# Layer 3 of a fused conv-and-sequence kernel: rows of the spatial map asked for one row block ahead, in image 0 on POOL's DMA queue

## The chip, the cores and the metric

The kernel runs on one core of a Trainium2 chip. The metric is the device time of one execution in microseconds (us), as the median of several executions. One execution is also recorded by the hardware profiler; its own time stands beside its span below.

## The reference, cut to what matters

Four layers are computed one after the other on a batch of 4 images of 96 channels and 64x64 pixels: a selective-scan sequence block, a depthwise convolution with a scan, a neighbourhood-attention block, and a deformable convolution with attention from the spectrum. The change touches the fourth alone:

```python
mag = jnp.abs(jnp.fft.rfft2(x, norm='ortho'))
ca = sigmoid(...)                # from mag: one factor per image and channel
sa = sigmoid(...)                # from mean, l2 and mag: one factor per image and pixel
y = x * ca * sa
magy = jnp.abs(jnp.fft.rfft2(y, norm='ortho')).mean(1, keepdims=True)
freq_e = jax.image.resize(magy, (b, 1, h, w), method='bilinear')
aux = jnp.concatenate([y, coord, freq_e], 1)
offset = _conv(aux, off_w, off_b, (1, 1))
gate = sigmoid(_conv(relu(_conv(aux, dg1_w, dg1_b, (1, 1))), dg2_w, dg2_b))
y_base = _conv(y, base_w, base_b, (1, 1))
sampled = _grid_sample_taps(y, px, py)      # 9 taps, bilinear, at pixel + offset
y_def = einsum('bcthw,oct->bohw', sampled, def_w) + def_b
z = (1 - gate) * y_base + gate * y_def
return relu(batch_norm(z) + x)
```

`sa` has one value per pixel and is the same for all channels.

## The kernel before, in words

An image lies in SBUF as 96 channels (partitions) by 4096 pixels. Layer 3 cuts it into 8 row blocks of 512 pixels (`NB` = 512, `NN` = 8), and numbers the blocks of all images m = 0 to 31. Nothing is reordered by a scheduler in this part: `tc.manual_schedule()` keeps each engine's instructions in the order in which the Python code emits them. Steps are written as generators, and two tables say which generator takes a step when.

The spatial map `sa` of an image is computed in pixel rows on 64 partitions (`sr_acc`), written to DRAM (`sa_d`, L1823), and read back by row blocks.

`attended(b, n)` makes row block n of y for image b. Its first step asks for the 512 values of the block, copied to 96 partitions (`sab`, L1883, 192 KB), and multiplies the block in place by `ca` and `sab` on DVE (L1885). Then `row_steps` transposes the block on PE (`tp`, L1610), copies it to SBUF (`xT`, L1615: on DVE in image 0, on ACT in the others), multiplies it by the row transform on PE (`fa`, L1626), and ACT copies the result to `f1` (L1634). After the copy to `xT`, eight DMAs on SyncE's queue (SP) write the block into a table in DRAM in which every pixel holds its four neighbours (L1892). `sab` has two buffers. `xT` has three, which it shares with `fT` (L1653, the copies of the column transform, `columns`; their matmuls are L1646 and L1657 and their sums L1663).

The first part of the layer is `front`. It runs a table of slots over the spectra of the four images, the maps, and `attended` of image 0: its blocks start at slots 42, 44, ... 56, with `columns` of image 2 and `described` of image 3 between them. POOL has nothing to do there.

The second part is a loop over u = 0 to 127, four u for each block m. It is called the gather stage here. For each u, POOL issues nine indirect DMAs (L2010, `gathered`) that fetch 128 pixels x 9 taps from the table, each 128 x 1536 B, into `sm` (three buffers). DVE weights and adds the neighbours (L2027 to L2031, `weighted`, for u-1), PE transposes the sums and ACT copies them (L2048 to L2051). `mixed(m)` multiplies them by the deformable weights (`yd`, L2060) and DVE combines the result (`z`, L2065). The addresses for block m+1 come meanwhile: `guides` (PE `go`, L1933, ACT L1946), `offsets` (PE L1954, DVE L1961 to L1990, with `om` on L1987), which POOL's next gathers wait for. `attended(b, n)` of images 1 to 3 is spread over this loop, one block every two u in the first half of image b-1. On DVE a cycle in that half has this order: offsets, attended, weighted, weighted, attended, weighted, z, weighted, offsets.

Of the kernel before, what the change touches and what calls it, by code (L numbers as in the profile page):

```python
# [10 lines left out]
F32 = mybir.dt.float32  # L11
I32 = mybir.dt.int32
AF = mybir.ActivationFunctionType
ALU = mybir.AluOpType
# [4 lines left out]
B, C, H, W = 4, 96, 64, 64  # L19
L = H * W  # L20
NB = 512
# [1808 lines left out]
def layer3(k, X, aux, out):  # L1830

    tc, nc, ins = k.tc, k.nc, k.ins
    with ExitStack() as es:
        wp = es.enter_context(tc.tile_pool(name="l3w", bufs=1))
        dram = es.enter_context(tc.tile_pool(name="l3d", bufs=1, space=DRAM))
        ca = wp.tile([C, B], F32, name="ca")
        sa_d = dram.tile([B, L], F32, name="sa_d")
# [26 lines left out]
        wk = es2.enter_context(tc.tile_pool(name="l3k", bufs=2))  # L1864
# [3 lines left out]
        NN, NJ = L // NB, 4  # L1868
# [2 lines left out]
        go, ix, cw, g, yb, sm, sd, sT = {}, {}, {}, {}, {}, {}, {}, {}  # L1871

        pairs = (("stp", "smm"), ("tp", "cv"))
        f1 = {}

        def attended(b, n, tags=None):

            table = tables[b % 2]
            s = slice(n * NB, n * NB + NB)
            if n == 0:  # L1880
                f1[b] = spec.begin()
            sab = wk.tile([C, NB], F32, name="sab")
            nc.sync.dma_start(sab, sa_d[b : b + 1, s].partition_broadcast(C))  # L1883
            y = X[b][:, s]
            nc.vector.scalar_tensor_tensor(y, y, ca[:, b : b + 1], sab, ALU.mult, ALU.mult)  # L1885
            yield
            for yT in spec.row_steps(f1[b], 4 * n, y, None, tags):
                if yT is not None:
                    for h2 in range(2):
                        for q in range(4):  # L1890
                            r, c = 8 * n + h2 + 1 - q // 2, 1 - q % 2
                            nc.sync.dma_start(  # L1892
                                table[r : r + 7 : 2, c : c + W, q].rearrange("r w c -> w r c"),
                                yT[64 * h2 : 64 * h2 + 64],
                            )
                yield
# [184 lines left out]
        def front(pool):  # L2081
# [7 lines left out]
            def chains(kind, b, ats):  # L2089
                for n, at in enumerate(ats):  # L2090
                    tags = pairs[at % 2]
                    if kind == "rows":
                        start(at, 3, described(b, n, pool, tags))
                    elif kind == "attended":
                        start(at, 4, attended(b, n, tags))
                    else:
                        start(at, 4, columns(b, FS[n], tags))
# [33 lines left out]
        with tc.manual_schedule():  # L2131
# [16 lines left out]
            for b in range(1, B):  # L2148
                u = NN * NJ * (b - 1)
                for n in range(NN):  # L2150
                    spread(2 * (u + 2 * n) + 1, 4, attended(b, n))
                u += 2 * NN + 1
                for i, f0 in enumerate(FS):
                    spread(2 * (u + i), 4, columns(b, f0))
                spread(2 * (u + len(FS) + 1), 4, frequency(b))
# [18 lines left out]
        for b in range(B):  # L2174
            for at in range(0, L, T):
                s = slice(at, at + T)
# [38 lines left out]
```

## Time and profile before

| | |
|---|---|
| median of 12 runs | 8195.92 us (8175.35 to 8217.66) |
| profiled execution, its own time | 8199.86 us |
| its span on the core | 8197.6 us |
| mean granted TensorE clock | 0.795 |
| busy PE, DVE, ACT, POOL | 71%, 71%, 48%, 57% of the span |
| layer 3, `front` up to the first gather | about 5640 to 6051 us of the span |
| gather stage | 6051 to 8117 us |
| `sab` requests on SP | 32, from 5823.8 to 7351.4 us |

A group line names the line of the code, the engine and the operation, what it writes and reads, how often, its busy time and mean, and the idle time of the engine just before it with what ended most of it. A wait line says who waited for whom: total us, number of times, longest. In a timeline a line starts with the start and the duration in us, and a bracket holds the idle time before it and what ended that. A releaser called "remote" is one that the profile could not put down to an instruction's end.

### The profile page before, as it was taken

Reading aid. Unit: us, or ns where it says so; the run is one execution under the profiler, and the core shown is the slowest. Engines: PE = TensorE matmul, PEld = TensorE weight load, DVE = VectorE, ACT = ScalarE, POOL = GpSimd, SP = SyncE. Lnnn points to the kernel's source line nnn. Section 1 sums busy time; section 2 is a strip of 40 time slices with the busy share of each in tenths; the row PEclk is TensorE's granted clock in tenths of the full one; section 3 lists DMA queues with packets and bytes.
Section 4 is the critical chain, followed back from the end, with each engine's and each line's share of the span. In section 5 each row is a group of like instructions: output and inputs, shape, how many; then the busy total and the mean of one; then the engine's idle time right before and its main releaser. Section 6 shows DMA issues by size and latency. Waiting matters only on the chain.

```text
span 8197.6 us, 76624 instructions
## 1 busy us (share of the span) xinstructions
PE 5826.7 (71%) x24090; PEld 2699.8 (33%) x24090; DVE 5788.8 (71%) x8127; ACT 3903.2 (48%) x7624; POOL 4693.4 (57%) x2915
## 2 busy tenths in 40 slices
PE   4777777777777776666788989897565566565553
PEld 1222222222222221422364646464542333233221
DVE  4999999999999998499763646454455565565555
ACT  4777776777677765344354646565321111111111
POOL 3888888888888887145442424243025555455453
PEclk8888888888888887777788888888677677777776
DMA  3322222332223332533200000000124344353333
GB/s 96 119 98 98 98 99 99 117 102 99 98 98 100 119 101 80 161 83 92 69 14 25 16 23 18 18 23 23 35 75 141 105 125 127 109 148 115 110 111 123
DMA packets 424411, 720.29 MB, mean 88 GB/s; under 512 B 188149, under 2 KB 190253, under 8 KB 419762
## 3 DMA queue, kind: packets, MB, share of 16 engines
q1 hardware_dynamic: 348710, 480.74, 19.0%
q0 software_dynamic: 73968, 227.47, 9.6%
q10 hardware_dynamic: 1328, 7.20, 0.2%
q8 instruction: 191, 3.13, 0.2%
q14 instruction: 214, 1.75, 0.1%
HBM read 567.04 MB, written 97.82 MB: 81 GB/s over the span
## 4 chain that ended last, share of the span: by engine, by line
PE 34%; DVE 26%; ACT 15%; issue 9%; another core or an unknown queue 8%; POOL 4%; DMA 3%; SPq 1%; DVEq 0%; ACTq 0%; POOLq 0%
DVE bt L604 6%; PE mm_ps L447 5%; DVE bt L577 3%; PE mm_ps L478 3%; PE yp L630 3%; PE sc_ps L1086 3%; ACT a_ps L588 3%; PE pT_ps L1135 2%; DVE prod L2027 2%; DVE sm L2028 2%; PE o_ps L1155 2%; POOL xc L472 2%; DVE lp L903 1%; PE yb_ps L1933 1%
## 5 line engine op out<-in xcount | busy, mean ns | idle before, releaser
L604 DVE TENSOR_TENSOR_SCAN bt<-a_ps,carry,bt 128x512 f32<-128x512 f32 x1536 | 1872.0, 1267 | 66.6 <-ACT a_ps L588 11.8
L613 POOL TENSOR_TENSOR bt<-bt,Cb 128x1536 f32<-128x1536 f32 x512 | 1758.3, 3444 | 200.1 <-ACT carry L612 178.7
L2010 POOL DMA_INDIRECT sm<-table,ix x1152 | 1097.5, 953 | 1319.2 <-DVE om L1987 493.9
L588 ACT ACTIVATE a_ps<-dR,w_l_A_log 128x512 f32<-128x512 f32 x1536 | 1039.9, 685 | 614.0 <-DVE bt L604 606.5
L577 DVE TENSOR_TENSOR bt<-xR,Bb 128x1536 f32<-128x1536 f32 x512 | 884.6, 1728 | 26.4 <-DMA xR<-spread 16.4
L2048 PE MATMUL sT_ps<-ident,sd 128*128 128x128 f32 (+1 forms) x896 | 223.0, 372 | 688.2 <-ACT sT L2049 344.5
L630 PE MATMUL yp<-bt,w_c_red 128*32 128x512 f32 x3072 | 596.1, 672 | 12.7 <-POOL bt L613 12.7
L570 PE MATMUL Bb<-dbl,w_c_seln 128*128 128x512 f32 x512 | 352.9, 777 | 326.3 <-DVE bt L577 326.3
L1123 POOL TENSOR_TENSOR p<-p,rs 128x392 f32<-128x392 f32 x384 | 312.0, 841 | 473.5 <-DVE rs L1121 404.8
L447 PE MATMUL mm_ps<-h,Wk 96*128 96x512 f32 x1024 | 481.2, 624 | 140.5 <-issue 87.3
L2065 DVE SCALAR_TENSOR_TENSOR z<-yd_ps,vec,yb 96x512 f32<-96x512 f32 x32 | 23.9, 746 | 530.3 <-remote 341.2
L2049 ACT COPY sT<-sT_ps 128x512 f32<-128x512 f32 (+1 forms) x256 | 122.0, 477 | 567.3 <-PE sT_ps L2048 241.5
L2048 PEld LDWEIGHTS sT_ps<-ident,sd 128*128 128x128 f32 (+1 forms) x896 | 132.7, 181 | 764.3 <-ACT sT L2049 373.8
L1110 ACT ACTIVATE p<-p,rs 128x196 f32<-128x196 f32 x768 | 342.7, 449 | 82.1 <-DVE rs L1100 81.9
L319 PE MATMUL bc_ps<-xs,w_l_bc 96*128 96x512 f32 x384 | 243.9, 769 | 184.1 <-DVE q L930 183.9
L447 PEld LDWEIGHTS mm_ps<-h,Wk 96*128 96x128 f32 x1024 | 198.1, 199 | 430.0 <-issue 430.0
L1946 ACT ACTIVATE go<-go_ps,w_l_go_b 18x512 f32<-18x512 f32 x32 | 21.7, 679 | 665.7 <-remote 503.9
L1933 PE MATMUL yb_ps<-X,w_l_base_w 96*128 96x504 f32 (+3 forms) x576 | 313.7, 710 | 0.3 <-ACT go L1947 0.3
L472 POOL TENSOR_TENSOR xc<-xc,gate 96x1024 f32<-96x1024 f32 x64 | 150.2, 2346 | 260.4 <-ACT carry L612 232.1
L1143 DVE COPY pT<-pT_ps 98x512 f32<-98x512 f32 x256 | 176.0, 687 | 148.8 <-PE pT_ps L1135 141.4
L2027 DVE TENSOR_TENSOR prod<-sm,cws 128x960 f32<-128x960 f32 (+1 forms) x256 | 270.8, 1058 | 6.7
L570 PEld LDWEIGHTS Bb<-dbl,w_c_seln 128*128 128x128 f32 x512 | 88.8, 217 | 552.8 <-DVE bt L577 492.9
(374 smaller groups left out, 13227.3 us busy)
## 6 DMA issues: line engine op xcount, KB each, us to landing
dR<-spread SPq DMA_DIRECT2D x384, 256.0 KB
xR<-spread SPq DMA_DIRECT2D x384, 256.0 KB
Cb<-out_states SPq DMA_DIRECT2D x256, 256.0 KB
spread<-w SPq DMA_DIRECT2D x128, 192.0 KB
spread<-dx SPq DMA_DIRECT2D x128, 192.0 KB
table<-xT SPq DMA_DIRECT2D x256, 96.0 KB
own<-vd SPq DMA_DIRECT2D x512, 36.8 KB
toep<-l_toep SPq DMA_DIRECT2D x12, 1536.0 KB
```

Of the source, the lines that this page charges most:

```text
L447: nc.tensor.matmul(p, Wk[:, i, t, hf], h[:, t : t + T], start=t == 0, stop=t == 3)
L570: nc.tensor.matmul(Bb, seln[:, nq], st["dbl"], start=True, stop=True)
L577: nc.vector.tensor_mul(bt, st["xR", hf, None], Bb.unsqueeze(1).to_broadcast([128, NG, T]))
L588: nc.scalar.activation(dec[n], st["dR", hf, q], AF.Exp, scale=A[:, i, nq, hf, q : q + 1])
L604: nc.vector.tensor_tensor_scan(t, dec.pop(n), t, carry_of(v)[:, q : q + 1], ALU.mult, ALU.add)
L613: nc.gpsimd.tensor_mul(bt, bt, st["Cb", nq].unsqueeze(1).to_broadcast([128, NG, T]))
L630: nc.tensor.matmul(st["yp", hf][32 * q : 32 * q + 32], red, bt[:, q], start=False, stop=nq == NQ - 1,)
L1110: nc.scalar.activation(ps[n][:, h, i], ps[n][:, h, i], AF.Exp, scale=-1.0, bias=rs[n][:, 0, h, i : i + 1], accum_out=rs[n][:, 1, h, i : i ...
L1933: nc.tensor.matmul(dv[:, r0:r1, c0:c1], w_[:, t], av[b][:ch, 8 * n + r0 + dy : 8 * n + r1 + dy, c0 + dx : c1 + dx], start=t == 4, stop=t == 8,
L2010: nc.gpsimd.indirect_dma_start(sm[u][:, t].rearrange("p q c -> p (q c)"), None, samples[m // NN % 2], bass.IndirectOffsetOnAxis(ap=ix[m][: ...
L2027: nc.vector.tensor_mul(p, v[:, :, 2:4], w_[:, :, 2:4])
L2048: nc.tensor.transpose(p[: e - 128 * q, q - q0], sf[:, 128 * q : e], k.ident)
```

## The change

A helper `fetch(b, n)` asks for the rows of one block. `attended(b, n)` now asks for block n+1 before it multiplies block n; with block 0 it asks for block 0 too. The requests of image 0 are issued by POOL's queue, those of images 1 to 3 by SP's as before. The multiplication takes the tile that was asked for earlier. The number of requests, their sizes and the buffers stay as they are.

```diff
-        f1 = {}
+        f1, sabs = {}, {}
+
+        def fetch(b, n):
+
+            t = sabs[b, n] = wk.tile([C, NB], F32, name="sab")
+            queue = nc.sync if b else nc.gpsimd
+            queue.dma_start(
+                t, sa_d[b : b + 1, n * NB : n * NB + NB].partition_broadcast(C)
+            )
...
             if n == 0:
                 f1[b] = spec.begin()
-            sab = wk.tile([C, NB], F32, name="sab")
-            nc.sync.dma_start(sab, sa_d[b : b + 1, s].partition_broadcast(C))
+                fetch(b, 0)
+            if n + 1 < NN:
+                fetch(b, n + 1)
             y = X[b][:, s]
-            nc.vector.scalar_tensor_tensor(y, y, ca[:, b : b + 1], sab, ALU.mult, ALU.mult)
+            nc.vector.scalar_tensor_tensor(
+                y, y, ca[:, b : b + 1], sabs.pop((b, n)), ALU.mult, ALU.mult
+            )
```

## The prediction

> **What bounds the kernel now.** I read the list of waits first, to see what the requests cost at all, and once more for the window of image 0 alone (5850 to 5960 us).
>
> ```profile
> DVE X L1885 <- DMA sab<-sa_d: 151.8, 23, 13.0
> POOL sm L2010 <- DVE om L1987: 493.9, 30, 33.2
> POOL sm L2010 <- DVE sd L2031: 125.7, 19, 13.8
> ```
>
> ```profile
> DVE X L1885 <- DMA sab<-sa_d: 60.6, 7, 8.9
> ```
>
> DVE stands 151.8 us before L1885 because the map's rows are not there; 60.6 us of it are seven waits in image 0, the other 91.2 us lie in the gather stage. The two POOL lines say that the gather queue stands still too, mostly for the addresses (`om`), less often for a free `sm` buffer (`sd`). Whether DVE's 91 us matter is decided there. Next the timeline of image 0, where one block gives way to the next.
>
> ```profile
> 5906.70 0.60 SPq L1883 DMA_DIRECT2D sab<-sa_d  x1
> 5909.94 0.75 DVE L1885 SCALAR_TENSOR_TENSOR X<-X,ca,sab 96x512 f32<-96x512 f32 x1 [8.56 <-DMA sab<-sa_d]
> 5910.74 0.90 PE L1610 MATMUL tp_ps<-ident,X 96*128 96x96 f32 x4 [4.85 <-DVE X L1885]
> 5911.69 0.56 DVE L1615 COPY xT<-tp_ps 128x384 f32<-128x384 f32 x1 [0.19 <-PE tp_ps L1610]
> 5912.27 5.24 SPq L1892 DMA_DIRECT2D table<-xT  x8
> 5917.56 0.60 SPq L1883 DMA_DIRECT2D sab<-sa_d  x1
> 5920.94 0.75 DVE L1885 SCALAR_TENSOR_TENSOR X<-X,ca,sab 96x512 f32<-96x512 f32 x1 [8.70 <-DMA sab<-sa_d]
> ```
>
> The request of a block stands in SP's queue behind the eight table stores of the block before (5.24 us of issuing), and its rows are usable 3.2 to 3.4 us after it is issued. All engines stand for that. The windows show how little else there is, against the stage after it:
>
> ```profile
> 5861.00:5945.00 84.00, 35.13 (x177) 30.00 (x178) 19.27 (x45) 9.91 (x25) 0.00 (x0) 0.60 0.37 83
> 6051.00:8117.00 2066.00, 1176.39 (x3419) 605.11 (x3417) 1170.06 (x1965) 287.73 (x647) 1097.28 (x1152) 0.71 0.43 122
> ```
>
> The columns are length, busy PE, PEld, DVE, ACT, POOL, clock, DMA share and GB/s. In the first, no engine is busy half the time. In the second POOL's 1097 us of 2066 are its issues. So last the timeline of the gather stage, one cycle with requests and one without (image 3 is done by then):
>
> ```profile
> 6108.95 0.95 POOL L2010 DMA_INDIRECT sm<-table,ix  x1 [13.00 <-DVE om L1987]
> ...
> 6163.06 0.68 ACT L1946 ACTIVATE go<-go_ps,w_l_go_b 18x512 f32<-18x512 f32 x1 [28.22 <-remote]
> ...
> 6170.18 0.94 POOL L2010 DMA_INDIRECT sm<-table,ix  x1 [11.52 <-DVE om L1987]
> ...
> 7879.36 0.95 POOL L2010 DMA_INDIRECT sm<-table,ix  x1 [19.41 <-DVE om L1987]
> ...
> 7930.19 0.75 DVE L2065 SCALAR_TENSOR_TENSOR z<-yd_ps,vec,yb 96x512 f32<-96x512 f32 x1 [26.09 <-remote]
> 7930.37 0.68 ACT L1946 ACTIVATE go<-go_ps,w_l_go_b 18x512 f32<-18x512 f32 x1 [25.64 <-remote]
> ...
> 7943.58 0.95 POOL L2010 DMA_INDIRECT sm<-table,ix  x1 [19.44 <-DVE om L1987]
> ```
>
> A cycle is 36 gathers at 1.25 us, 44.8 us, and then a pause. ACT's `go` starts about 5 us after the last gather has been issued (6158.66 and 6163.06; 7924.14 and 7930.37), though PE's `go` matmuls are recorded as over 13 to 15 us earlier. What holds PE's signal back the trace does not say ("remote"). If `z` was free before, the next gathers start 7.1 us after `go` (a cycle of 61.2 us in the first); if `z` comes free with `go`, one `weighted` (8 us) still stands between, and it is 13.2 us (64.2 us in the second). So the cycle without any request to wait for is the longer one.
>
> **The change, part by part.** Requests of image 0. Eight issues leave SP's queue (0.61 us each) and go to POOL, whose queue is idle for 350.7 us up to the first gather, so nothing is queued behind them. PE, DVE and ACT keep their instructions in the old order. `sab` has two buffers, so the request of block n+1 waits on POOL for the multiplication of block n-1 and must have landed by that of n+1, two blocks later.
>
> The price of such a request on POOL is in no row. The nearest are a gather's issue (0.95 us, 25 of 1152 above 1.0, longest 1.41) and the landing of `sab` by SP (3.4 us at most): 4.8 us together at worst, against two blocks of at least 5.3. I take it as hidden; uncovered, it would cost no more than the wait of today.
>
> Here a rule speaks against the change. The gathers' longest issue beside DVE work was 0.46 us above the usual. The Trainium skill, SBUF — State Buffer, "SBUF: two separate sides", says that GpSimd cannot write descriptors while DVE runs a copy in a two-port mode, and advises SP's or ACT's queue. It would make a request late by one DVE instruction; the longest recorded here beside the blocks is 0.75 us, which the lead covers too.
>
> What is late next, block by block. Block 1 follows block 0 at once: 8.76 us gone. In block 2 the wait of 8.57 us goes, but the next map's matmuls, rl and sigmoid (L1804 to L1822) come onto the path; I take 7.5. Blocks 3 to 7 now take 10.95 us each (`xT` at 5889.67 and 5944.44). Three things bound a block then. SP still issues eight stores: 5.25 us plus 0.05. PE's chain from `tp` to the second `fa` is 6.0 us at half clock (5899.88 to 5905.89) and 5.1 at the faster one (5932.65 to 5937.77). And `fT` stands on DVE ahead of `xT`, sharing its three buffers: it waits for the stores of two blocks before, 0.58 us to the issue, 5.25 of issue, at most 3.3 to land, 0.55 for itself, so 9.7 us in two blocks. I take 5.6 us per block, between SP and PE: 5 x 5.35 = 26.8. Together 8.8 + 7.5 + 26.8 = 43 us. The ends are 30 (a block of 8.2 us, if the stores land late) and 45 (5.3). After image 0 the same chain of PE, DVE and ACT leads to the first gather with no queue of its own, so all of it arrives.
>
> Requests of images 1 to 3. Their place in SP's queue is the one that the request of the block before had, so no store is later. The first block's wait stays. L1885 finds its rows, and DVE's two `weighted` after it end about 6 us earlier, the next by 11. That frees `sm` sooner: the 2 to 8 us that POOL stands for a buffer in each of the twelve cycles that hold later requests go (POOL's timeline), so the 36 gathers take 44.8 us instead of 47 to 53. But the length of a cycle is then that of the cycles without waits. There are nine whole ones (the two that hold only a first block, 64.25 and 60.74, and seven at the end, 64.20 to 64.35): mean 63.9. The twelve cycles with later requests (from 6108.95 to 6360.90, 6638.40 to 6889.78 and 7164.18 to 7410.80, first gather to first gather) take 750 us, 62.5 each. I take 12 x 1.37 = +16 us, a loss. The ends are all at 58.2 us, as in the first cycle, which has no `z` (6050.78 to 6108.95): -52; and all at 64.25: +21.
>
> The profiled execution took 8199.86 us; 8199.86 - 43 + 16 = 8173. It lay 3.9 above the median of the runs, so against that: 8169.
>
> **The rivals.** A: with `sm` free early, `yd` runs before the signals are held, `z` is free before `go`, and the cycles fall to 58.2 us. For it: that first cycle. Against: the cycles at the end have `yd` as early (28 us into the cycle) and are held. 8196 - 43 - 52 = 8101 at its full size.
>
> B: image 0 gains little, since POOL's requests land late or hold PE's signals as the gathers do. For it: requests of this kind are not in the trace. Against: eight requests are not 36 in a row, and in the first 15 us of a gather run PE's signals are prompt. With 16 to 30 us left of 43 it is 8182 to 8196: no change. A change that does not do what it says falls here too.
>
> C, slower: taking the waits away moves the twelve cycles into the order of those with column steps (cycles 5, 6, 13, 14, 21, 22: 66.0 to 68.8, mean 67.4), where POOL stands 7 to 14 us for a buffer because DVE waits for ACT. 12 x 4.9 = +59, so 8196 - 43 + 59 = 8212. It decides from a mean cycle of 66.1 us on. Against it: those DVE waits belong to steps that the attended cycles lack.
>
> **How the numbers follow.** My case 0.64, A 0.12, B 0.14, C 0.10. About 0.2% (16 us) is what a measurement of this kernel can tell from no change, so faster means below 8179.5. My case with its ends gives 8143 to 8187 and is mostly faster; A is faster, B the same, C slower. Faster 0.70, same 0.18, slower 0.12. The range 8135 to 8190 holds my case, most of B and the start of A.
>
> **What would show it.** In the profile after: no wait for `sab` before the multiplication in blocks 1 to 7, the table stores of image 0 nearly back to back on SP, the first gather at about 6008 instead of 6050.8, no POOL wait on `sd` in the attended cycles and their lengths at 61 to 64. A first gather later than 6021 would break the first step, a mean attended cycle above 65 or below 61 the second.

## The result, and the profile after

The changed kernel took 8297.5 us (median of 11 runs, 8282.0 to 8323.6), the kernel before 8194.6 (46 runs); the ratio is 1.0132 (95%: 1.0119 to 1.0146). Forecast were 8169 us and a gain. The profiled execution after has a span of 8300.5 us, 102.9 more than before.

The experiments ran in five sets, each on a chip of its own and each with runs of the kernel before. In two sets that kernel took 8196 and 8173 us as here, in three others 7600, 7595 and 7600; every ratio below is therefore taken within a set, and where times of two sets stand side by side the text says so.

First the waits. Of the lines shown before, DVE's wait for `sab` is gone. POOL's for `sd` is gone in the twelve cycles with later requests; the 83.4 us that are left (first line) lie in the cycles with column steps. The other lines grew in their place:

```profile
POOL sm L2021 <- DVE sd L2042: 83.4, 7, 14.0
POOL sm L2021 <- DVE om L1998: 702.8, 31, 33.2
DVE z L2076 <- PE yd_ps L2071: 554.5, 21, 39.8
ACT sT L2060 <- remote: 411.4, 47, 26.3
```

POOL waits 702.8 us for addresses instead of 493.9 (lines after the change are 11 higher). DVE waits 554.5 us for `yd` (150.0 before; in all it stands 811.7 us before `z`, 530.3 before the change, the rest mostly put down to "remote"), and ACT 411.4 us for something that the profile cannot name before it copies the transposed sums (216.3 before). Image 0 did what was forecast:

```profile
5871.64 33.70 SPq L1903 DMA_DIRECT2D table<-xT  x48
5875.33 0.74 DVE L1894 SCALAR_TENSOR_TENSOR X<-X,ca,sab 96x512 f32<-96x512 f32 x1
5876.36 0.51 POOL L1880 DMA_DIRECT2D sab<-sa_d  x1 [3.29 <-DVE X L1894]
5878.62 0.56 DVE L1615 COPY xT<-tp_ps 128x384 f32<-128x384 f32 x1 [1.75 <-PE fb_ps L1657]
5879.10 0.74 DVE L1894 SCALAR_TENSOR_TENSOR X<-X,ca,sab 96x512 f32<-96x512 f32 x1
```

The multiplication no longer has a bracket: it follows its predecessor at once. A block comes every 3.8 us here instead of 10.9, and six blocks' stores leave SP in one string. The windows say the same, and where the time went:

```profile
5861.00:5945.00 84.00, 65.11 (x475) 58.47 (x474) 51.68 (x150) 33.62 (x78) 2.05 (x4) 0.77 0.39 86
6000.00:8221.00 2221.00, 1145.90 (x3420) 591.02 (x3417) 1168.63 (x1965) 287.22 (x647) 1093.94 (x1152) 0.70 0.40 114
```

In 84 us of image 0 PE and DVE are now busy 65 and 52 us (35 and 19 before). The gather stage does the same work (POOL 1094 us, DVE 1169) in 2221 us instead of 2066. By POOL's timeline the twelve cycles with later requests take 902.6 us instead of 750.0, the other nineteen 1273.9 instead of 1271.3. One of the twelve, from 6135.71 on:

```profile
6148.39 0.60 PE L2059 MATMUL sT_ps<-ident,sd 128*128 128x128 f32 x4
...
6167.25 0.58 ACT L2060 COPY sT<-sT_ps 128x512 f32<-128x512 f32 x1 [18.44 <-remote]
6174.97 0.37 ACT L2060 COPY sT<-sT_ps 128x256 f32<-128x256 f32 x1 [7.14 <-issue]
6175.94 1.19 PE L1626 MATMUL fa_ps<-w_c_dw,xT 128*96 128x132 f32 x4 [7.15 <-ACT xT L1615]
6179.72 0.95 POOL L2021 DMA_INDIRECT sm<-table,ix  x1 [0.30 <-issue]
6186.65 0.37 ACT L1634 COPY f<-fa_ps 96x264 f32<-96x264 f32 x1 [10.76 <-remote]
...
6190.50 7.27 PE L2071 MATMUL yd_ps<-sT,w_l_def_w 128*128 128x512 f32 x14
6197.80 0.75 DVE L2076 SCALAR_TENSOR_TENSOR z<-yd_ps,vec,yb 96x512 f32<-96x512 f32 x1 [36.32 <-PE yd_ps L2071]
6205.45 0.68 ACT L1957 ACTIVATE go<-go_ps,w_l_go_b 18x512 f32<-18x512 f32 x1 [14.18 <-PE go_ps L1944]
6212.01 0.94 POOL L2021 DMA_INDIRECT sm<-table,ix  x1 [31.35 <-DVE om L1998]
```

PE's transposes are over at 6148.99, and ACT copies them at 6167.25. The next result of PE (6168.8) reaches ACT at 6174.97, the one after (6177.1) at 6186.65. That is 6.0 us after the last gather has been issued, and from there every handover (one engine's result to the engine that reads it) takes a microsecond again. Only then can `yd` (7.3 us), `go` (7.8) and the addresses follow, all behind the gathers: 76.3 us.

Before the change the same steps mostly ended early, because POOL stood at +11 us (it waited for a buffer that DVE, late for `sab`, had not freed). In the twelve cycles these stands are not alike. Two of them, with `yd` of the same cycle:

```profile
6186.17 0.95 POOL L2010 DMA_INDIRECT sm<-table,ix  x1 [4.77 <-DVE sd L2031]
6195.76 7.75 PE L2060 MATMUL yd_ps<-sT,w_l_def_w 128*128 128x512 f32 x14
...
6246.33 0.95 POOL L2010 DMA_INDIRECT sm<-table,ix  x1 [1.01 <-DVE sm L2030]
6274.71 7.53 PE L2060 MATMUL yd_ps<-sT,w_l_def_w 128*128 128x512 f32 x14
```

The first cycle starts at 6170.18, the second at 6234.34. In nine of the twelve the stand at +11 is 2.2 to 4.8 us long, and `yd` ends at +31 to +34; in three it is 1.0 us or missing, and `yd` ends at +48 to +49. After the change none of the twelve has it, and `yd` ends at +58 to +64. The theory taken to the chip: **PE's signals come late in a long unbroken run of gathers; the waits that the change removes were breaks in that run.**

### The profile page after: what moved, and what is told of

It reads as the page before. It is cut to its first block, busy times and chain, and to the rows that moved or that the text cites. A ratio compares the mean times of both kernels' runs of the same rounds, so it can differ in the third digit from the quotient of the medians.

```text
span 8300.5 us, 76635 instructions
## 1 busy us (share of the span) xinstructions
PE 5788.1 (70%) x24090; PEld 2679.3 (32%) x24090; DVE 5783.5 (70%) x8127; ACT 3902.1 (47%) x7624; POOL 4692.5 (57%) x2923
## 4 chain that ended last, share of the span: by engine, by line
PE 38%; DVE 22%; ACT 15%; another core or an unknown queue 9%; issue 8%; POOL 4%; DMA 2%; SPq 0%; DVEq 0%; ACTq 0%; POOLq 0%
DVE bt L604 5%; PE mm_ps L447 5%; DVE bt L577 3%; PE yp L630 3%; PE mm_ps L478 3%; PE sc_ps L1086 2%; ACT a_ps L588 2%; PE yb_ps L1944 2%; PE yd_ps L2071 2%; PE pT_ps L1135 2%; PE o_ps L1155 2%; POOL xc L472 2%; PE go_ps L1944 2%; DVE lp L903 1%
## 5 line engine op out<-in xcount | busy, mean ns | idle before, releaser
L2021 POOL DMA_INDIRECT sm<-table,ix x1152 | 1094.5, 950 | 1245.5 <-DVE om L1998 702.8
L577 DVE TENSOR_TENSOR bt<-xR,Bb 128x1536 f32<-128x1536 f32 x512 | 884.7, 1728 | 23.6 <-DMA xR<-spread 16.3
L630 PE MATMUL yp<-bt,w_c_red 128*32 128x512 f32 x3072 | 599.8, 676 | 12.7 <-POOL bt L613 12.7
L2076 DVE SCALAR_TENSOR_TENSOR z<-yd_ps,vec,yb 96x512 f32<-96x512 f32 x32 | 23.9, 747 | 811.7 <-PE yd_ps L2071 554.5
L2060 ACT COPY sT<-sT_ps 128x512 f32<-128x512 f32 (+1 forms) x256 | 121.9, 476 | 722.7 <-remote 411.4
L1626 PE MATMUL fa_ps<-w_c_dw,xT 128*96 128x132 f32 x512 | 115.5, 371 | 231.3 <-issue 134.8
```

The lines of the kernel that those rows point to most:

```text
L577: nc.vector.tensor_mul(bt, st["xR", hf, None], Bb.unsqueeze(1).to_broadcast([128, NG, T]))
L630: nc.tensor.matmul(st["yp", hf][32 * q : 32 * q + 32], red, bt[:, q], start=False, stop=nq == NQ - 1,)
L2021: nc.gpsimd.indirect_dma_start(sm[u][:, t].rearrange("p q c -> p (q c)"), None, samples[m // NN % 2], bass.IndirectOffsetOnAxis(ap=ix[m][: ...
```

## The experiments

Cycle lengths are from first gather to first gather on POOL; "twelve" is the mean of the cycles with later requests, "free" that of the last seven whole ones, without steps of another image.

| set | kernel | us | ratio to before (95%) | twelve | free |
|---|---|---|---|---|---|
| 1: before 8195.9 | image 0 alone ahead | 8134.0 | 0.9930 (0.9903 to 0.9957) | 61.7 | 64.1 |
| | images 1 to 3 alone ahead | 8347.7 | 1.0184 (1.0160 to 1.0207) | 74.9 | 64.1 |
| | image 0 alone, on SP | 8147.7 | 0.9943 (0.9921 to 0.9965) | 63.0 | 63.5 |
| | change + 5.2 us pause | 8137.2 | 0.9930 (0.9907 to 0.9954) | 61.8 | 64.0 |
| 2: before 8172.7 | change + 2.3 us pause | 8090.1 | 0.9897 (0.9880 to 0.9915) | 59.0 | 62.9 |
| | change + pause after the run | 8286.1 | 1.0145 (1.0128 to 1.0162) | 73.9 | 63.1 |
| | image 0 alone + POOL waits for go | 8266.5 | 1.0115 (1.0097 to 1.0133) | 74.8 | 63.0 |
| | change + POOL waits for go | 8269.7 | 1.0121 (1.0104 to 1.0138) | 74.8 | 62.4 |
| 3: before 7600.3 | change + one memset | 7511.3 | 0.9887 (0.9863 to 0.9912) | 45.7 | 45.1 |
| | change + five after each nine | 7798.8 | 1.0270 (1.0245 to 1.0295) | 54.7 | 54.5 |
| | change + two after each nine | 7626.9 | 1.0036 (1.0021 to 1.0052) | 49.0 | 48.9 |
| | change + one after each third | 7624.8 | 1.0026 (1.0012 to 1.0039) | 48.9 | 48.6 |
| 4: before 7594.7 | the change itself | 7494.0 | 0.9881 (0.9857 to 0.9905) | 45.3 | 45.2 |
| 5: before 7600.3 | image 0 alone ahead | 7555.0 | 0.9943 (0.9921 to 0.9964) | 46.7 | 45.2 |

**The two halves apart.** Each kernel keeps the ahead request for some images and asks in the block's own step for the rest:

```diff
+            if b == 0:                # second kernel: b > 0
+                if n == 0:
+                    fetch(b, 0)
+                if n + 1 < NN:
+                    fetch(b, n + 1)
+            else:
+                fetch(b, n)
```

> Image 0 alone asks one block ahead, on POOL's queue; images 1 to 3 ask for a block in its own step, as before. In the changed kernel the first gather came 51 us earlier (5999.7 for 6050.8) and the twelve gather cycles with later requests 153 us longer in sum (902.6 for 750.0). If these are two separate effects, this kernel keeps the first alone: first gather at 6000, the twelve cycles at 62 to 63 us, 8194.6 - 51 = 8144. If the requests on POOL's queue, or the earlier start, are what lengthens the cycles, they stay at 75 and the time is near 8297.

> Images 1 to 3 alone ask one block ahead, on SP's queue; image 0 asks as before. If the two effects are separate, first gather at 6051, twelve cycles at 75 us, 8194.6 + 153 = 8347. If the requests on POOL's queue lengthen the cycles: cycles at 62 to 63 and no more than 8195.

Both came as two separate effects would have it (8134 for 8144, 8348 for 8347): -62 us and +152 us in one set, beside -51 and +153 us read from the traces before and after. Image 0's requests on POOL cost the gather stage nothing (61.7 us a cycle).

**The queue.** As the first, with `queue = nc.sync` for all.

> As the kernel with image 0 alone ahead, but its requests stay on SP's queue. A request for block n+1 then stands behind the stores of block n-1 and goes out at about the time of block n's copy, so it lands 3.3 us later, partly after DVE could use it. If the place in SP's queue is what counts, half of the 51 us is kept: first gather near 6020, 8165 (8150 to 8180). If asking ahead alone is enough and the queue does not matter: first gather at 6000, 8144.

Measured 8147.7, nearer to "the queue does not matter". From block 0's multiplication to the first gather it takes 159.6 us, against 200.8 before, 152.0 in the change and 147.6 with image 0 alone on POOL. Asking ahead gives 41 us, POOL's queue 8 to 12 more: SP's requests still leave DVE six waits, 20.0 us (60.6 before). I had put the price of SP's queue too high.

**A pause in the run.** The change, with idle writes on POOL in the twelve cycles:

```diff
                     gathered(u)
+                    if u % 4 == 0 and u // 4 in (1, 2, 3, 4, 9, 10, 11, 12, 17, 18, 19, 20):
+                        for _ in range(11):        # 5: half pause; 1: one memset
+                            nc.gpsimd.memset(zero, 0.0)
```

> The changed kernel, with a pause written into POOL's instructions: in the twelve attended cycles eleven small memsets of an idle tile (of zeros, to zero) between the ninth and the tenth gather, an estimated 4.5 us, about as long and at the same place as POOL's wait for a buffer in the kernel before. Theory 'pause': PE's signals come late in a long unbroken run of gathers, and the wait for a buffer broke the run; with a pause the attended cycles fall from 75 to 61 to 65 us, time 8297 - 903 + 12 x 63 = 8150. Rival 'order': the earlier multiplication brings the block's transposes and copies ahead of the sums on PE and ACT, and that alone delays yd and go, whatever POOL does; then the cycles stay at 75 or grow by the pause to 80, time 8297 to 8350.

Measured 8137.2: 160 us below the change's own time in the result (0.9930 of before instead of 1.0132), by making POOL do more. The same steps in the kernel with the long pause, in the cycle from 6068.50 on:

```profile
6079.53 5.17 POOL L2175 MEMSET zero<- 66x384 f32 x11
...
6082.27 0.59 ACT L2060 COPY sT<-sT_ps 128x512 f32<-128x512 f32 x1 [0.24 <-PE sT_ps L2059]
...
6086.11 1.20 PE L1626 MATMUL fa_ps<-w_c_dw,xT 128*96 128x132 f32 x4 [0.46 <-ACT f L1634]
...
6089.53 8.71 PE L2071 MATMUL yd_ps<-sT,w_l_def_w 128*128 128x512 f32 x14
...
6098.28 0.75 DVE L2076 SCALAR_TENSOR_TENSOR z<-yd_ps,vec,yb 96x512 f32<-96x512 f32 x1 [4.01 <-PE yd_ps L2071]
```

The order of instructions is the change's, but PE and ACT answer each other in a microsecond, and `z` comes 29.8 us into the cycle instead of 62.1. The rival that puts it to the order alone is out.

> The changed kernel with a pause of half the length at the same place: five memsets (0.47 us each, 2.35 us by the kernel with eleven) after the ninth gather of the twelve attended cycles. In all traces so far a late signal of PE arrives 4.1 to 4.4 us after POOL begins to stand. If a pause must be that long to release anything, 2.35 us release nothing: cycles at 75 to 78, time 8297 to 8335. If a pause lets signals through in proportion, about half of the 160 us comes: cycles near 68, time 8217.

> Control: the same eleven memsets in the same twelve cycles of the changed kernel, but after the last nine gathers, where POOL stands for addresses for 30 us anyway. If the pause inside the run is what helps, nothing changes: cycles at 75, 8297. If memsets help by themselves (a write of POOL that flushes something), cycles fall towards 62 and the time to 8137.

The half pause missed both expectations, on the good side: 59.0 us a cycle, 8090.1 in a set whose kernel before is 8172.7. I had read the length from how long a signal already late takes to come through (4.1 to 4.4 us). This pause lies at +11, before any is late, and 2.3 us are enough to keep them prompt for the steps that follow, up to PE's `yd`, which ends at +27 to +30 in all twelve (`yd`'s own signal is late again in four, by 2.9 to 19 us); the rest of the 5.2 us was only paid (run ends at +47.5 instead of +50.2, cycle 59.0 instead of 61.8). The stands before the change point the same way: 2.2 us were enough in two cycles, 1.0 us was not in two. The control has its memsets where POOL stands anyway: they change nothing (73.9 us a cycle), so it also stands for the change itself in this set. Of the versions run where signals are late it has the lowest ratio to before, 0.9897 beside 0.9930 of image 0 alone; the two come from different sets, and their intervals overlap a little.

**A wait in place of the pause.** Before the last nine gathers of every cycle POOL reads `go`:

```diff
+                    if u % NJ == 3 and u // NJ + 1 < B * NN:
+                        seen = wk.tile([128, 1], F32, name="seen")
+                        nc.gpsimd.tensor_copy(seen[64:82], go[u // NJ + 1][64:82, :1])
                     gathered(u)
```

> The kernel with image 0 alone ahead, and in every cycle POOL first copies one column of go (18 values) before the last nine of the 36 gathers. POOL then stands at +33.8 until go is there. Theory 'pause': go's matmuls end at +35 to +42 in the free cycles, the stand lets their signal through about 4.4 us after it begins, so go comes at 39 instead of 51, the last gathers end near 51, and the addresses are ready before that: cycles of 51 to 56 instead of 64, 31 cycles, 8134 - 31 x 10 = 7820 (7750 to 7950). Rival: signals are late for another reason than the gathers, and POOL waits for go as long as ACT did, to +51; the last nine gathers then end at +62 and the cycles grow to 64 to 70: 8134 to 8320.

> The changed kernel (images 1 to 3 one block ahead too) with the same copy of go before the last nine gathers of every cycle. Theory 'pause': the attended cycles, 75 in the changed kernel, are cut as soon as POOL stands: PE and ACT still have to pass the block's steps, yd and go (about 25 us) after the stand begins at +33.8, so 33.8 + 25 + 11 = 70 in the twelve cycles and 51 to 56 in the free ones: 8297 - 12 x 5 - 10 x 10 = 8130 (8000 to 8200), behind the kernel that has image 0 alone ahead. Rival: no cycle gets shorter, 8297 or more.

Both missed: 8266.5 and 8269.7. The first cycle went as forecast, 50.9 us in both. From then on the next 27 gathers follow the last nine without a stand, and the run of 36 merely starts elsewhere (waits of the kernel with image 0 alone; its lines are 4 higher again):

```profile
POOL seen L2178 <- ACT go L1961: 643.4, 31, 30.8
ACT yb L2013 <- remote: 478.7, 18, 36.8
```

ACT now waits for PE's `yb` at the head of the cycle (in the cycle from 6064.01 on, matmuls over at 6071.30, `yb` at 6086.34), and POOL stands up to 30 us for `go`. So POOL's long stand between two cycles had been the time in which PE's first handovers of each cycle were prompt.

**How long and how often.** These were to find the shortest break that helps:

> The changed kernel with a single memset (0.47 us) after the ninth gather of the twelve attended cycles. With five (2.3 us) these cycles took 59 us instead of 75. If the length of the stand counts, 0.5 us is too little: cycles near 75, 8297. If any other instruction of POOL between the gathers is enough, whatever its length: cycles at 57 us, 8090 - 12 x 1.9 = 8067.

```diff
                     gathered(u)
+                    for _ in range(5):             # 2 in the next kernel
+                        nc.gpsimd.memset(zero, 0.0)
```

> The changed kernel with five memsets (2.3 us) after every nine gathers, in all 32 cycles. Theory: PE's signals turn late only after 11 us or more of gathers without a break, so none turns late; go is there at about +38, the addresses before the last nine gathers end, and POOL's own work is the cycle: 4 x (11.25 + 2.35) = 54.4 us, some of the column cycles longer. The stage falls from 2036 us (the kernel with five memsets in twelve cycles) to about 1780: 8090 - 256 = 7830 (7780 to 7950). Rival: a break shifts the late signals without shortening them, and every break is paid: cycles of 64 + 7, 8300.

> As the kernel with five memsets after every nine gathers, but with two (0.94 us). If such a break is long enough, POOL's work is 4 x 12.2 = 48.8 us a cycle and the time 8090 - (2036 - 1620) = 7670 (7650 to 7850). If it is too short, the signals are late in every cycle and POOL has no stand between the cycles in which they could come: 8250 or more, with cycles of 66 to 75.

```diff
                 nc.gpsimd.indirect_dma_start(...)   # one gather of nine
+                if t % 3 == 2:
+                    nc.gpsimd.memset(zero, 0.0)
```

> The changed kernel with one memset (0.47 us) after every third gather, in all cycles: 5.6 us a cycle, about the sum of the kernel with two or three after every nine, but no break longer than 0.8 us. If the mean rate of gathers is what makes the signals late, this is as good as longer breaks: cycles of 51 to 52 us, about 7720. If a break has to have a length: 8300 or more.

None of this was answered. The kernel before took 7600 us here, and no signal was late in any of the four (of the handovers from PE to ACT and DVE in the gather stage none took over 0.1 us; in the profile after 93 took over 2): each cycle is POOL's own time, 45 us with one memset and more by just the memsets (54.5 with 4 x 2.3 us). Times near the forecast of one theory (7799 for 7830) are not evidence for it, since no break was needed.

**The change without late signals.**

> The changed kernel as it is. In the last set the kernel before took 7600 us instead of 8196 and every gather cycle of the four kernels was POOL's own 45 to 55 us, with no signal of PE late: that chip does not show the late signals at all. If this set's kernel before is near 8190 (late signals), the changed kernel is at 1.013 of it; if it is near 7600, the changed kernel gains what image 0 gives and a little more, 0.988 to 0.993 of it, cycles of 45 us.

Measured 7494.0, 0.9881 of 7594.7. This set had no late signals either, so the two kernels with breaks told nothing new (7806.7 and 7618.4):

> The changed kernel with five memsets (2.3 us) after every nine gathers. Where signals are late (the kernel before near 8190), theory 'run length': no signal turns late, cycles of 54.5 us as in the last set, 7800 (7780 to 7950). Rival 'breaks only shift': 8250 to 8350. Where they are not late: 7799 again.

> The changed kernel with one memset after every third gather, in all cycles, 48.6 us a cycle in the last set. Where signals are late: if the mean rate of the gathers makes them late, 7630 to 7700; if a break must be 2 us long, 8250 or more. Where they are not: 7625 again.

The waits and the stage of the change on this chip:

```profile
ACT go L1957 <- PE go_ps L1944: 452.6, 32, 15.8
POOL sm L2021 <- issue: 329.9, 1083, 0.3
```

```profile
5982.00:7429.00 1447.00, 1112.95 (x3441) 569.64 (x3440) 1190.18 (x1992) 290.89 (x656) 1096.21 (x1152) 0.81 0.60 174
```

There is no "remote" among the stage's waits, and POOL no longer waits for `om`: its idle time is its own issuing, and the same work that took 2221 us takes 1447. Up to the first gather the two chips differ by 18 us (5981.6 and 5999.4). The granted clock differs too (0.81 and 0.70 in the stage), but PE's busy time by 33 us only, so the clock alone does not make the 774.

> Image 0 alone ahead, once more. Where signals are late (the kernel before near 8190): 0.993 of it again. Where they are prompt (near 7595): POOL's own 45 us are the cycle, and each of the twelve attended cycles still holds DVE's waits for the rows and POOL's stand of about 4 us for a buffer, 49 to 50 us; so of the 101 us that the whole change saves there, image 0 gives 51 and the twelve cycles the other 50: 7545 (0.9935 of before).

Measured 7555.0. Image 0 gives 45 us of the 101 that the change gave in set 4 (51 were expected); the other part did not lie where I put it. The twelve cycles are only 1.4 us longer than in the change of that set (46.7 for 45.3, 17 us in sum), and 31 us are in the other nineteen, mostly the column cycles (47.6 to 52.2 us for 45.0 to 45.7). That DVE, busy for 1190 of the stage's 1447 us, carries the lost time over to them is likely, but no run shows it. The waits for the rows are 98.5 us in this kernel:

```profile
DVE X L1898 <- DMA sab<-sa_d: 98.5, 22, 6.8
```

The last two kernels were to find the break again, but this set was one without late signals too (one memset 7503.4, five after each nine 7803.5, before 7600.3):

> The changed kernel with one memset (0.47 us) after the ninth gather of the twelve attended cycles. Where signals are late: if the length of the break counts, cycles near 75 and 1.012 of before; if any break does, 57 us and 0.985 of before. Where they are prompt: 7511 again.

> The changed kernel with five memsets (2.3 us) after every nine gathers, all cycles. Where signals are late: 0.95 to 0.97 of before (cycles of 54.5 us) if a run of 11 us is too short for signals to turn late; 1.00 or more if breaks only shift them. Where they are prompt: 1.028 of before again.

## Why the prediction was wrong

**Image 0 (-43; ends 30 and 45): right in kind, too small.** From block 0's copy `xT` to block 7's it took 84.1 us before (5860.36 to 5944.44) and takes 34.4 (5857.75 to 5892.11). Blocks 1 and 2 gave 16.0 of the 49.7, by the forecast 16.3. Blocks 3 to 7 gave 33.7 instead of 26.8: a block is 4.2 us, not the 5.6 that I took between SP and PE. SP does need 5.6 us for eight stores (33.70 for 48), but with three buffers it may run behind, and does, up to 13 us after the last copy, while nobody waits for it. PE's chain of 5.1 to 6.0 us was no bound either: blocks follow each other faster than that, so the chains of two blocks overlap. All but a microsecond of it reached the first gather (200.8 to 152.0 us from block 0's multiplication). Of the price of a request on POOL, bounded by 4.8 us, the trace shows 0.51 us of issuing; the landing is not recorded, but no multiplication of image 0 waited for its rows. The rule that I had weighed against it (the Trainium skill, SBUF — State Buffer, "SBUF: two separate sides") would have made requests late, and none was late here: the eight issues took 0.51 to 0.58 us. Whether DVE ran a copy of that kind just then no run shows.

**Gather stage (+16; ends -52 and +21): this step failed.** In the twelve cycles POOL's stands for a buffer went, as said, and the 36 gathers take 44.7 to 45.0 us. What failed is the next sentence, that "the length of a cycle is then that of the cycles without waits", mean 63.9. Those nine have little to hand over between PE and ACT ahead of `yd`: their transposes are at most a few microseconds late each (up to 8), and `yd` still ends at +27 to +39. The twelve have the block's copy and its two transforms in that order as well; each handover costs 6 to 18 us instead of one (in the cycle shown), and `yd` ends at +58 to +64. The term, forecast as 12 x 1.37 = +16, is 12 x 12.7 = +153. The prediction's own sign for this step, a mean cycle above 65 us, came with 75.2. Rows of before warned of it: the cycles from 6496.11, 7025.53 and 7544.21 also have 44.8 us of unbroken gathers and other steps ahead of `yd` (`frequency`), with `yd` at +64.7, and take 78.0, 77.9 and 78.0 us. I had named the mechanism in the timeline, used it for `go` alone, and picked as model the cycles in which little is left for it to hold. By the three other rows the term would have been 12 x 15.5 = +186, and the forecast a loss. What is held in those three looks different, though:

```profile
6517.45 0.26 PE L1674 MATMUL fe_ps<-f,pick 96*33 96x64 f32 x1 [1.92 <-issue]
...
6548.81 0.21 ACT L1682 COPY fe<-fe_ps 33x64 f32<-33x64 f32 x1 [36.95 <-PE fe_ps L1674]
```

There PE itself is slow: of 66 matmuls in a row, which wait for nothing that the profile shows, eleven come 2 to 3.5 us apart, until 3 us after the last gather. The 66 take 37.5 us in this cycle, in the changed kernel of set 4 6.1. So the three rows would have given the right sign, but not by late signals alone.

Two smaller things in the prediction do not hold. PE's signals are not prompt for the first 15 us of a run: before the change too, copies of ACT are late for results that PE had at +12. And the lower end of 8143 does not follow from the terms beside it: 8196 - 45 - 52 is 8099.

**The rivals.** C had the right sign and the wrong mechanism: it let POOL stand for buffers, which it does not in the twelve cycles, and its price of 4.9 us a cycle is 12.7. A is what happens where signals are prompt, with 45 us a cycle; B did not occur.

So the change itself saves 1.2% where PE's signals are prompt, and loses 1.3% where they are late. Shown: the breaks in POOL's run decide it (pause, control and halves in sets 1 and 2). Open: what holds the signals (the gathers' transfers, something in PE's own queue, or the recording of its instructions: no run separates them); why the result and sets 1 and 2 show it and sets 3 to 5 do not (each set is one chip at one time, and those with late signals are the earlier ones, so chip and time cannot be told apart); and how short a break may be (the stands before the change put it between 1.0 and 2.2 us at +11, in two cycles each, and no kernel tested it where signals are late).

## What to carry to other kernels

A wait can do work: before removing one, ask what its stand lets through, and who gets the engine's queue, the memory or the signals in that time. A model cycle has to contain the same handovers as the one that it stands for, not only lack the same waits. And where a trace says "remote", measure on a second chip before tuning against it: where signals are late the change with the half pause had the lowest ratio of the kernels run (0.9897), and where they are not the change without any pause is as good as the best (0.9881; with one memset 0.9887 and 0.9873).

## What the hardware showed

- In sets 1 and 2, and in both profiles shown, signals of PE to ACT and DVE reach them up to 26 us late from about 11 us on in a run of gathers issued every 1.25 us (up to 34 in the kernels that wait for `go`); those still held when POOL stops come within about 6 us. PE itself mostly goes on: in a cycle of before (7879.36) `yd`'s and `go`'s 32 matmuls are through at +28.1 and +35.8, and `z` starts at +50.8. But in the `frequency` cycles its own matmuls come 2 to 3.5 us apart. ACT's signals to PE are prompt (in the changed kernel, in the middle of a run, a copy ends at 6167.83 and the matmul that waits for it starts at 6167.89).
- 2.3 us without gathers at +11 keep PE's signals prompt for the steps up to the end of `yd` at about +28; `yd`'s own signal was late again in four of twelve cycles.
- In sets 3 to 5 the same gathers at the same pace (1.25 us) delay nothing (no handover of PE over 0.1 us): 45.1 us a cycle instead of 64.1, 600 us of 8200 for the kernel before.
- A plain request on POOL's queue is issued in 0.51 us beside busy DVE, a memset of 66x384 values in 0.41.
